# Seven moves in the schedule of an attention kernel: padding later, dividing sooner, one output product moved to the front of its place

## The chip, the cores and the metric

The program runs on one core of one Trainium2 chip. The metric is device time in microseconds (us), the median of three runs. Five engines work side by side, each in the order of its own instruction list: TensorE (PE; its weight loads are shown as PEld), VectorE (DVE), ScalarE (ACT), GpSimd (POOL), and SyncE (SP), which issues most transfers. [...] The order in which the program emits instructions is therefore the order in which each engine must do them, and a wait at the head of one list holds up everything behind it. Lines are cited as L and a number, which is the line of the kernel before.

## What is computed

The input is x of shape (4, 256, 48, 48) in 32-bit floats: four images of 256 channels and 2304 positions. Four layers follow, each added to its input; the first three read a group normalisation of it.

```python
x = x + L0(gn(x))   # 8-head attention over 2304 positions, q and k normalised; w_out, bias
x = x + L1(gn(x))   # gate: 3x3 max pool, blur with stride 3 to 16x16, depthwise taps, sigmoid, upsampled
x = x + L2(gn(x))   # one-head non-local attention, then a batch norm over all images
x = x + L3(x)       # channel gate, depthwise 3x3 convolution, instance norm, leaky relu

# the core of L0, for each image and head
sim  = einsum('bhdi,bhdj->bhij', q, k) * 10.0
out  = einsum('bhij,bhdj->bhid', softmax(sim), v)
y    = einsum('oc,bchw->bohw', w_out, out) + b_out

# the core of L1
t    = blur_pool(max_pool_3x3(gn(x)), stride=3)          # 16x16
gate = sigmoid(bn(dw(t, w_h1) + dw(t, w_v1) + diagonal taps of t))
y    = gn(x) * upsample(gate)
```

Layer 1 becomes 81 taps of a 16x16 tile that has a border of zeros (the padded tile).

## The kernel before, the parts concerned

Layer 0 is 16 phases, one for each image b and pair of heads p. A phase is six units of 384 query positions each, and a unit is nine groups of two blocks of 128 keys: 54 groups to a phase. Layer 2 follows with four phases of 27 groups. All other work (projections of the next pair, layer 1 of the image before, statistics) is given out to the groups. Within a group the emission order is this:

```python
for t, (u, g, st) in enumerate(groups):
    for j in range(g * G, (g + 1) * G):
        scores(u, j)                  # PE: scores (L238) into one of 2 "sc" tiles; ACT: exp (L244) -> pt
    if prev is not None:
        add_up(*prev)                 # DVE and POOL: row sums of exp (L284, L269)
    do(due, t)                        # small steps that are due, e.g. invert, divide
    do(fills, t)                      # PE work at fixed groups, sorted by the number it comes with
    ...
    for lane in st["others"]:         # generators: layer 1, group norms, follow
        gen, n, a, z, done, ready = lane
        until = -(-n * (st["at"] + 1 - a) // (z - a))
        clock["final"] = final = st["at"] == z - 1
        while final or (done < until and t >= ready and not ends):
            wait = next(gen, None)    # a yielded number: groups to wait
            if wait is None:
                break
            done, ready = done + 1, t + wait
    if prev is not None:
        ... weigh(pu, j)              # PE: exp times values (L258), of the group before
        if pg == NG - 1:
            last(pu, t)               # ends a unit
    prev = (u, g)
```

The end of a unit, counted in groups after its last weighing:

```python
AT_TOTAL, AT_FOLD, AT_INVERT, AT_DIVIDE, AT_AFTER = 3, 2, 6, 10, 11

def last(u, t):
    take(u)                                                      # ACT: copy out of PSUM
    ...
    todo = [
        (fills, AT_TOTAL, lambda: total(u)),                     # PE, ACT, SP: sums to a small tile l6
        (due, AT_FOLD, lambda: fold(u, nc.gpsimd)),              # POOL (L335)
        (due, AT_INVERT, lambda: invert(u)),                     # DVE (L311, L312), SP: rinv to 128 rows
        (due, AT_DIVIDE, lambda: divide(u, nc.gpsimd)),          # POOL: o = o * rinv (L339)
    ]
    after = AT_AFTER
    todo += [(fills, after, fn) for fn in u["after"]]            # the two output products
```

The group with number 2 in each unit (11 after the end of the last one) is the place of the 128-row products. The projection of the next pair stands there with the numbers 1, 2 and 3, and the output products beside it:

```python
def out_proj(b, p, c, pair, o):
    def part(k):
        ps = pj_tile()                                           # one of 2 "pj" banks
        nc.tensor.matmul(ps[:, :SL], lhsT=wo[...], rhs=o["o"], start=True, stop=True)        # L568
        xs = X[b][:, k, cols]
        nc.vector.scalar_tensor_tensor(xs, ps[:, :SL], pair["bo"][...], xs, ALU.add, ALU.add)  # L573
    return [((2.5, 4)[k], lambda k=k: part(k)) for k in range(NK)]

def chunk(s):              # qk: PE L502, evicted by ACT; values: PE L518, evicted by ACT
    def end():
        qk(s, 1)
        if s + 2 < NCH:
            fetch(s + 2)
    return [(1, lambda: qk(s, 0)), (2, lambda: values(s)), (3, end)]
```

Every `pj_tile()` takes the next of two banks in turn and has to wait until the reader of the one before last is done with it.

Layer 1 of image b runs beside the attention of image b + 1 and a little beyond it:

```python
TURNS, ROUND, HASTE = (2, 2, 3, 5, 6, 8), -1, -2      # groups of a unit in which a step may be taken
ROUND_TURNS = {ROUND: (2, 5, 8), HASTE: (2, 4, 6, 8)}

def padded(k, norm, res):
    pd = lp.tile([P, AS + 2 * PAD, AS + 2 * PAD], F32, tag="pd", name="pd")
    nc.gpsimd.memset(pd, 0.0)                                                    # POOL L724
    rs64 = lp.tile([P, 1], F32, tag="rs64", name="rs64")
    nc.vector.tensor_scalar(rs64, norm["rs"][:, k : k + 1], 1.0 / 64.0, ...)     # DVE L726
    nc.scalar.activation(pd[inner], res["blur"], AF.Identity, bias=..., scale=rs64)  # ACT L727
    return pd

def strips(b, k, norm, res):
    haste = HASTE if (b, k) == (NX - 1, NK - 1) else ROUND
    pd = padded(k, norm, res)
    ...
    products(0)            # ACT: 5 taps (L747)
    yield haste
    products(1)            # ACT: 4 taps
    yield haste
    for n, taps in enumerate(ROUNDS):      # 20 rounds
        ...                # ACT: products(n + 2); DVE: tensor_reduce (L765)
        yield haste

def l1_all(b):
    ...                    # statistics of the group norm, first half of the maxima
    for k in range(NK):
        if k:
            res = {}
            yield from maxima(b, k, res)       # DVE: 12 steps of max and blur, the last L708 to L715
        yield from strips(b, k, norm, res)
        yield from gated(b, k, norm, res)
        ...
    yield from gn(b, norm2, [1])               # statistics for layer 2

def follow(start, slices, norm):               # projection of the last image of layer 2
    while "nb" not in norm:
        yield 1
    start()                                    # PE L889, L895 on norm["nb"]
    yield 1
    for c in range(L2C):
        ...
```

And where the phases are set up:

```python
if (b, p) == (2, 0):
    for s in range(NSL):
        work.setdefault(s + 2 * NG, []).append(lambda s=s: send(s))      # X[0] to DRAM
        work.setdefault(s + 3 * NG, []).append(lambda s=s: receive(s))   # image 3 into its place
if b > 1 and p == 0:
    others.append((l1[b - 2], 10**6, 0, 2 * NG))     # rest of layer 1 of the image before last
```

Of the kernel before, what the change touches and what calls it, by code (L numbers as in the profile page):

```python
# [17 lines left out]
NK = 2  # L18
# [46 lines left out]
NG = JB // G  # L65
# [9 lines left out]
def usual_path(  # L75
# [15 lines left out]
    def pj_tile():  # L91
        return ps_pj.tile([P, 512], F32, tag="pj", name="pj")
# [5 lines left out]
    NX = B - 1  # L98
# [259 lines left out]
        nc.vector.tensor_tensor(lmin[:, 0:1], lmin[:, 0:1], two[:, 1:2], ALU.min)  # L358

    due, fills, clock = {}, {}, {}  # L360
    AT_TOTAL, AT_FOLD, AT_INVERT, AT_DIVIDE, AT_AFTER = 3, 2, 6, 10, 11

    def last(u, t):

# [197 lines left out]
    def out_proj(b, p, c, pair, o):  # L562

        cols = slice(c * SL, (c + 1) * SL)

        def part(k):
            ps = pj_tile()
            nc.tensor.matmul(  # L568
                ps[:, :SL], lhsT=wo[:, p, k * P : (k + 1) * P], rhs=o["o"], start=True,
                stop=True,  # L570
            )
            xs = X[b][:, k, cols]
            nc.vector.scalar_tensor_tensor(  # L573
                xs, ps[:, :SL], pair["bo"][:, k : k + 1], xs, ALU.add, ALU.add
            )

        return [((2.5, 4)[k], lambda k=k: part(k)) for k in range(NK)]

    def l0_unit(b, p, c, pair):
        hold = {}  # L580

        def o_tile():
            hold["o"] = op.tile([P, SL], F32, tag="o", name="o")
            return hold["o"]

        return {
            "pt": {}, "qc": slice(c * SL, (c + 1) * SL), "paired": PAIRED,
            "soon": b == B - 1 and p == NPAIR - 1 and c == NCH - 1,
            "scale": 1.0, "of": pair, "o": o_tile,
            "after": out_proj(b, p, c, pair, hold),  # L590
        }
# [60 lines left out]
    TURNS, ROUND, HASTE = (2, 2, 3, 5, 6, 8), -1, -2  # L652
    ROUND_TURNS = {ROUND: (2, 5, 8), HASTE: (2, 4, 6, 8)}

    def paced(gen):

        at, count, wait, turns = -9, 0, 0, TURNS
        while True:
            t, slot = clock["t"], clock["slot"]
            count = count if t == at else 0  # L660
            if not clock["final"] and (t < at + wait or count >= turns.count(slot)):
                yield 1
                continue
            wait = next(gen, None)
            if wait is None:
                return
            at, count = t, count + 1
            turns = ROUND_TURNS.get(wait, TURNS)
            yield 0
# [51 lines left out]
    def padded(k, norm, res):  # L721

        pd = lp.tile([P, AS + 2 * PAD, AS + 2 * PAD], F32, tag="pd", name="pd")
        nc.gpsimd.memset(pd, 0.0)  # L724
        rs64 = lp.tile([P, 1], F32, tag="rs64", name="rs64")
        nc.vector.tensor_scalar(rs64, norm["rs"][:, k : k + 1], 1.0 / 64.0, None, ALU.mult)  # L726
        nc.scalar.activation(  # L727
            pd[:, PAD : PAD + AS, PAD : PAD + AS], res["blur"], AF.Identity,
            bias=norm["nb"][:, k : k + 1], scale=rs64,
        )  # L730
        return pd

    def strips(b, k, norm, res):


        haste = HASTE if (b, k) == (NX - 1, NK - 1) else ROUND
        pd = padded(k, norm, res)

        bufs = [
            lp.tile([P, L1_BUF], F32, tag=tag, name="prod").rearrange("p (n s) -> p n s", s=NT + 1)  # L740
            for tag in ("t1", "t2", "t3")
        ]

        def products(n):
            for i, t in enumerate(ROUNDS[n]):
                dr, dc = TAPS[t]
                nc.scalar.activation(  # L747
                    bufs[n % 3][:, :, min(n, 1) + i].rearrange("p (r c) -> p r c", c=AS),
                    pd[:, PAD + dr : PAD + dr + AS, PAD + dc : PAD + dc + AS],
                    AF.Identity, scale=wt[:, k, t : t + 1],  # L750
                )

        products(0)
        yield haste
        products(1)
        yield haste
        for n, taps in enumerate(ROUNDS):
            last = n == len(ROUNDS) - 1
            if n + 2 < len(ROUNDS):
                products(n + 2)  # L760
            to = bufs[(n + 1) % 3][:, :, 0]
            if last:
                res["acc"] = lp.tile([P, AS, AS], F32, tag="l1acc", name="l1acc")
                to = res["acc"].rearrange("p r c -> p (r c)")
            nc.vector.tensor_reduce(  # L765
                to, bufs[n % 3][:, :, : min(n, 1) + len(taps)], AX.X, ALU.add
            )
            yield haste
# [246 lines left out]
    def l1_all(b):  # L1015

        norm, norm2 = norms1[b], norms2[b]
        norm2["st"] = small.tile([P, NK, NSL, 6], F32, tag="gn_st2", name="gn_st2")
        start = clock["t"]
        ahead = gn(b, norm)  # L1020
        for _ in range(NSL - 1):
            yield next(ahead)
        res = {}
        tops = maxima(b, 0, res)
        for _ in range(6):
            yield next(tops)

        while clock["t"] < start + NG + 2:
            yield 1
        yield from ahead  # L1030
        yield from tops
        for k in range(NK):
            if k:
                res = {}
                yield from maxima(b, k, res)
            yield from strips(b, k, norm, res)
            yield from gated(b, k, norm, res)
            if k == 0:
                for s in range(NSL):
                    nc.vector.bn_stats(norm2["st"][:, k, s, :], X[b][:, k, s * SL : (s + 1) * SL])  # L1040
                    if s % 2:
                        yield 0
        yield from gn(b, norm2, [1])
# [42 lines left out]
    l1 = [paced(l1_all(b)) for b in range(NX)]  # L1086
# [3 lines left out]
    def part(gen, n, last):  # L1090
        while n > 0 or last:
            wait = next(gen, None)
            if wait is None:
                return
            n -= 1
            yield wait
# [6 lines left out]
    def follow(start, slices, norm):  # L1103

        while "nb" not in norm:
            yield 1
        start()
        yield 1
        for c in range(L2C):
            while clock["t"] in taken:  # L1110
                yield 1
            for _, fn in slices[c] + slices[c + L2C]:
                fn()
            yield 1
# [6 lines left out]
    def send(s):  # L1121
        cols = slice(s * SL, (s + 1) * SL)
        nc.sync.dma_start(x_out[:, :, cols], X[0][:, :, cols])

    def receive(s):
        cols = slice(s * SL, (s + 1) * SL)
        nc.sync.dma_start(X[NX][:, :, cols], xv[:, :, NX, cols])
# [10 lines left out]
    for i, (b, p) in enumerate(order):  # L1138
        work, others = {}, []
        if i + 1 < len(order):  # L1140
            new = projs[i + 1]
            work[0] = [new["start"]]
            for s in range(NCH):
                work[NG * s + AT_CHUNK] = new["chunk"](s)
            work[NG + AT_CHUNK].append(new["out_bias"])
            for slot, fn in zip((n - 5, n - 3, n - 2, n - 1), new["scale"]):
                work[slot] = [fn]
            if i + 2 < len(order):
                work[n // 2] = [projs[i + 2]["prefetch"]]
                work[NG * (NCH - 1) + AT_CHUNK].append(projs[i + 2]["norms"])  # L1150
        else:
            start, slices = project2(0, norms2[0], twos[0])
            work[1] = [start]
            for s in range(NSL):
                work[NG * s + AT_CHUNK] = slices[s]
        if (b, p) == (2, 0):
            for s in range(NSL):
                work.setdefault(s + 2 * NG, []).append(lambda s=s: send(s))
                work.setdefault(s + 3 * NG, []).append(lambda s=s: receive(s))
        if (b, p) == (0, 0):  # L1160
            others.append((tap_weights(), WEIGHT_TICKS, 2, n - 2))
        if b > 0:
            end = n - 2 if (b, p) == (B - 1, NPAIR - 1) else n + 1
            others.append((l1[b - 1], 10**6, 2 if p == 0 else 0, end))
        if b > 1 and p == 0:
            others.append((l1[b - 2], 10**6, 0, 2 * NG))
        if (b, p) == (B - 1, NPAIR - 1):
            others.append((part(ahead, L1_AHEAD, False), L1_AHEAD, n - L1_AHEAD - 3, n))
        if p == 1 and b + 1 < B:
            others.append((gn(b + 1, norms0[b + 1]), GN_TICKS, 0, n - 2))  # L1170
        phases.append(([l0_unit(b, p, c, pairs[b][p]) for c in range(NCH)], work, others))

    n = L2C * NG
    for b in range(B):
        work, others = {}, []
# [1257 lines left out]
```

## Time and profile before

| quantity | before |
|---|---|
| median of 3 runs | 3723.43 us |
| lowest and highest | 3720.27 and 3728.46 us |
| span of the profiled run | 3718.2 us |
| PE busy | 3525.9 us, 95% |
| DVE busy | 2513.3 us, 68% |
| ACT busy | 2358.7 us, 63% |
| POOL busy | 1417.3 us, 38% |
| mean granted TensorE clock | 0.978 |

Busy time is how long an engine had an instruction of the program in it. The granted clock is the share of its full speed that TensorE was given. In lists of groups the columns are line, engine, operation, written and read tiles, shape and count, then busy time, mean nanoseconds of one, and the idle time of that engine just before them with what ended it. In a timeline each row is one instruction or a merged run of equal ones: start, duration, engine, line, operation, tiles, count, and in brackets the idle time before it and what ended it. A list of waits has the waiting engine, tile and line, an arrow to what it waited for, and then the total in us, how often, and the longest.

### The profile page before, as it was taken

To read this page: it belongs to the slowest core of one execution; us is meant where nothing else is said; L and a number is where in the kernel's file an instruction comes from. 1 tells how busy PE (TensorE), PEld (TensorE's weight loads), DVE (VectorE), ACT (ScalarE), POOL (GpSimd) and SP (SyncE) were. 2 spreads that over 40 slices of the span, in tenths; PEclk is the share of its full clock that TensorE was granted. 3 is DMA by queue.
4 is the path that set the end of the run, shared out by engine and by line. 5 is a ranking of instruction groups with operands and counts; after the bars stand their busy time and mean duration, and the time that the engine had idled before them with its cause. 6 is when DMAs were issued, how large, how long until landed. Compare 5 with 4: busy or idle time off the path is not lost.

```text
span 3718.2 us, 86544 instructions
## 1 busy us (share of the span) xinstructions
PE 3525.9 (95%) x36330; PEld 1770.1 (48%) x36330; DVE 2513.3 (68%) x3203; ACT 2358.7 (63%) x3819; POOL 1417.3 (38%) x900
## 2 busy tenths in 40 slices
PE   7999999999999999999999999999999999989685
PEld 4444545544445444444454444444444445655343
DVE  2455555476768666866686668666877886575687
ACT  5665666656776677567766775677678655545353
POOL 2333333333334333333343334333433456664242
PEclk9999999999999999999999999999999999999797
DMA  4111111111111111121111111111111100000001
GB/s 140 21 25 21 26 21 25 21 25 21 25 21 26 20 25 21 33 64 25 21 25 21 25 21 24 22 25 21 25 16 24 18 4 8 6 7 5 26 29 74
DMA packets 114591, 97.89 MB, mean 26 GB/s; under 512 B 56224, under 2 KB 111632, under 8 KB 112400
## 3 DMA queue, kind: packets, MB, share of 16 engines
q1 hardware_dynamic: 111728, 91.27, 12.9%
q8 instruction: 286, 4.69, 0.5%
q10 hardware_dynamic: 2464, 1.00, 0.1%
q14 instruction: 113, 0.93, 0.1%
HBM read 59.33 MB, written 11.80 MB: 19 GB/s over the span
## 4 chain that ended last, share of the span: by engine, by line
PE 76%; DVE 13%; issue 4%; ACT 2%; DMA 2%; POOL 2%; SPq 0%; DVEq 0%; POOLq 0%; ACTq 0%
PE sc L238 29%; PE av L258 29%; PE pj L502 7%; DVE acc L284 4%; PE pj L568 3%; PE pj L518 3%; DVE sc L1423 2%; DMA rinv<-rinv 1%; PE pj L291 1%; DVE av L1423 1%; PE pj L809 1%; POOL half L269 1%; DVE z L1472 1%; PE pj L925 1%; DVE gn_st L174 1%
## 5 line engine op out<-in xcount | busy, mean ns | idle before, releaser
L244 ACT ACTIVATE pt<-sc 128x768 f32<-128x768 f32 x1944 | 1477.3, 812 | 843.0 <-PE sc L238 833.8
L269 POOL TENSOR_TENSOR half<-pt 128x768 f32<-128x768 f32 x477 | 950.9, 1994 | 1619.4 <-ACT pt L244 1567.9
L238 PE MATMUL sc<-q,k 64*64 64x384 f32 x13824 | 1286.9, 488 | 31.9 <-ACT pt L244 29.4
L258 PE MATMUL av<-pt,v 64*64 64x384 f32 x13824 | 1285.1, 487 | 0.0
L284 DVE TENSOR_TENSOR acc<-acc,pt 128x768 f32<-128x768 f32 x792 | 876.1, 1106 | 103.2 <-ACT pt L244 20.6
L238 PEld LDWEIGHTS sc<-q,k 64*64 64x64 f32 x13824 | 516.2, 134 | 657.1 <-issue 515.9
L258 PEld LDWEIGHTS av<-pt,v 64*64 64x64 f32 x13824 | 517.5, 134 | 595.1 <-issue 558.8
L284 DVE TENSOR_TENSOR acc<-acc,half 128x768 f32<-128x768 f32 x459 | 476.9, 1039 | 296.7 <-POOL half L269 295.3
L573 DVE SCALAR_TENSOR_TENSOR x<-pj,bo,x 128x384 f32<-128x384 f32 x192 | 118.5, 618 | 566.1 <-PE pj L568 565.9
L502 PE MATMUL pj<-xs,w 128*128 128x384 f32 (+1 forms) x768 | 298.2, 512 | 1.7 <-issue 1.7
L747 ACT ACTIVATE prod<-pd,wt 128x256 f32<-128x256 f32 x486 | 280.4, 742 | 0.2
L339 POOL TENSOR_TENSOR o<-o,rinv 128x384 f32<-128x384 f32 x95 | 120.6, 1270 | 370.4 <-DMA rinv<-rinv 341.6
L502 PEld LDWEIGHTS pj<-xs,w 128*128 128x128 f32 x768 | 131.8, 190 | 153.9 <-issue 53.5
L258 PE MATMUL av<-pt,qv 64*64 64x384 f32 x1728 | 176.5, 500 | 0.0
L238 PE MATMUL sc<-qv,kd 64*64 64x384 f32 x1728 | 172.0, 490 | 3.9 <-ACT pt L244 3.9
L568 PE MATMUL pj<-o,wo 128*128 128x384 f32 x384 | 156.4, 492 | 16.4 <-POOL o L339 12.1
L765 DVE TENSOR_REDUCE prod<-prod 128x256 f32<-128x1280 f32 x114 | 168.7, 1480 | 0.0
L518 PEld LDWEIGHTS pj<-w,xs 128*128 128x128 f32 x1152 | 143.9, 192 | 25.9 <-issue 0.6
L278 DVE TENSOR_TENSOR acc<-pt 128x768 f32<-128x768 f32 x99 | 123.6, 1248 | 30.6 <-ACT pt L244 30.5
L518 PE MATMUL pj<-w,xs 128*128 128x128 f32 x1152 | 144.1, 275 | 0.0
L508 ACT ACTIVATE k<-pj,bias 128x384 f32<-128x384 f32 x96 | 55.7, 580 | 137.8 <-PE pj L502 137.3
L238 PEld LDWEIGHTS sc<-qv,kd 64*64 64x64 f32 x1728 | 80.2, 136 | 69.0 <-issue 53.0
(226 smaller groups left out, 2688.3 us busy)
## 6 DMA issues: line engine op xcount, KB each, us to landing
xs<-in_x_dram SPq DMA_DIRECT2D x96, 384.0 KB
rinv<-rinv SPq DMA_DIRECT2D x208, 94.5 KB
x<-in_x_dram SPq DMA_DIRECT2D x6, 1152.0 KB
out_dram<-x SPq DMA_DIRECT2D x6, 1152.0 KB
l<-row SPq DMA_DIRECT2D x416, 1.5 KB
w<-in_wqkv_dram SPq DMA_DIRECT2D x32, 192.0 KB
rinv<-ls SPq DMA_DIRECT2D x208, 1.5 KB
x_out<-x SPq DMA_DIRECT2D x6, 384.0 KB
```

Source lines behind the costliest of these rows:

```text
L238: nc.tensor.matmul(ps[c * D : (c + 1) * D, h, :SL], lhsT=u["of"]["k"][r, j0 : j0 + D], rhs=u["of"]["q"][r, u["qc"]], start=True, stop=True,)
L244: nc.scalar.activation(pt, ps[:, :, :SL], AF.Exp, scale=u["scale"])
L258: nc.tensor.matmul(u["av"][h * D : (h + 1) * D, half, :SL], lhsT=value(u, j, h)[r], rhs=pt[r, h, :], start=j == 0, stop=j == JB - 1,)
L269: nc.gpsimd.tensor_add(half, pts[0], pts[1])
L278: nc.vector.tensor_add(u["acc"], ready[0], ready[1])
L284: nc.vector.tensor_add(u["acc"], u["acc"], term)
L339: eng.tensor_mul(o, o, u["rinv"])
L502: nc.tensor.matmul(ps[:, :n], lhsT=at["w"][:, k, t, :], rhs=xs[s][:, k, :n], start=k == 0, stop=k == NK - 1,)
L518: nc.tensor.matmul(ps[:, i * P : (i + 1) * P], lhsT=xs[s][:, k, i * P : (i + 1) * P], rhs=at["w"][:, k, 2, :], start=k == 0, stop=k == NK - 1,
L568: nc.tensor.matmul(ps[:, :SL], lhsT=wo[:, p, k * P : (k + 1) * P], rhs=o["o"], start=True, stop=True,)
L747: nc.scalar.activation(bufs[n % 3][:, :, min(n, 1) + i].rearrange("p (r c) -> p r c", c=AS), pd[:, PAD + dr : PAD + dr + AS, PAD + dc : PA ...
L765: nc.vector.tensor_reduce(to, bufs[n % 3][:, :, : min(n, 1) + len(taps)], AX.X, ALU.add)
```

## The change

It moves seven things and computes the same. The sums of a unit are inverted, and its output divided, one group sooner. The first of the two output products goes to the front of the 128-row place. Layer 1 waits three groups between the last step of a blur and the padded tile made from it, so that ACT does not meet a tile that is not there yet. Because this makes layer 1 longer, the last layer-1 image goes at the quicker pace for both channel halves, and the rest of an earlier image may reach nine groups further into the next image; the reload of X[0] moves along by nine groups. Last, the projection for the last image of layer 2 starts two groups after its norm is there.

```diff
-    AT_TOTAL, AT_FOLD, AT_INVERT, AT_DIVIDE, AT_AFTER = 3, 2, 6, 10, 11
+    AT_TOTAL, AT_FOLD, AT_INVERT, AT_DIVIDE, AT_AFTER = 3, 2, 5, 9, 11
@@ out_proj
-        return [((2.5, 4)[k], lambda k=k: part(k)) for k in range(NK)]
+        return [(4 * k, lambda k=k: part(k)) for k in range(NK)]
@@ strips
-        haste = HASTE if (b, k) == (NX - 1, NK - 1) else ROUND
+        haste = HASTE if b == NX - 1 else ROUND
@@ l1_all
                 yield from maxima(b, k, res)
+
+            yield 3
             yield from strips(b, k, norm, res)
@@ follow
         while "nb" not in norm:
             yield 1
+        yield 2
         start()
@@ phases
-                work.setdefault(s + 3 * NG, []).append(lambda s=s: receive(s))
+                work.setdefault(s + 4 * NG, []).append(lambda s=s: receive(s))
@@
-            others.append((l1[b - 2], 10**6, 0, 2 * NG))
+            others.append((l1[b - 2], 10**6, 0, 3 * NG))
```

## The prediction

> **What bounds the kernel now.** I read the engines' busy shares first, then the list of TensorE's waits, then timelines around the longest. TensorE is busy for 3525.9 of 3718.2 us, and in an ordinary group it does scores and weighing back to back in 2.6 us. So only TensorE's idle stretches, and the slow clock after them, can be won.
>
> TensorE's own waits:
>
> ```profile
> engine line waited for: us in total, times, longest us
> PE sc L238 <- ACT pt L244: 33.3, 9, 4.8
> PE pj L568 <- POOL o L339: 12.1, 7, 2.9
> PE pj L889 <- DVE gn_nb L201: 7.2, 1, 7.2
> PE pj L192 <- DVE gn_sq L189: 5.3, 4, 2.0
> ```
>
> Six of the nine waits for exp lie in layer 0 and are 28.9 us of the 33.3, each 4.8 us. TensorE around one of them:
>
> ```profile
> 1648.15 1.47 PE L238 MATMUL sc<-q,k 64*64 64x384 f32 x16
> 1649.44 1.47 PE L258 MATMUL av<-pt,v 64*64 64x384 f32 x16
> 1655.72 2.84 PE L238 MATMUL sc<-q,k 64*64 64x384 f32 x16 [4.81 <-ACT pt L244]
> 1658.34 2.79 PE L258 MATMUL av<-pt,v 64*64 64x384 f32 x16
> ```
>
> The reader is to see the wait and that the next two runs take 2.8 us instead of 1.47: the granted clock is 0.75 over the 13.8 us from the wait's start, which is 6.9 us at half speed. ACT at the same time:
>
> ```profile
> 1647.22 0.87 ACT L300 COPY row<-pj 128x384 f32<-128x384 f32 x2
> 1651.63 0.60 ACT L727 ACTIVATE pd<-blur,gn_nb,rs 128x256 f32<-128x256 f32 x1 [3.54 <-DVE rs L726]
> 1652.27 2.76 ACT L747 ACTIVATE prod<-pd,wt 128x256 f32<-128x256 f32 x5
> 1654.84 1.53 ACT L244 ACTIVATE pt<-sc 128x768 f32<-128x768 f32 x2
> ```
>
> ACT stands 3.54 us before the padded tile, because VectorE reaches the tiny scale late, behind two steps of the blur and the row sums. Exp stands behind the tile and its five products.
>
> The second thing to read is the 128-row place while VectorE is behind. TensorE there, and VectorE there:
>
> ```profile
> 1200.32 1.47 PE L238 MATMUL sc<-q,k 64*64 64x384 f32 x16
> 1201.72 1.56 PE L502 MATMUL pj<-xs,w 128*128 128x384 f32 x4
> 1203.12 1.50 PE L518 MATMUL pj<-w,xs 128*128 128x128 f32 x12
> 1204.45 0.81 PE L568 MATMUL pj<-o,wo 128*128 128x384 f32 x2
> 1205.19 1.56 PE L502 MATMUL pj<-xs,w 128*128 128x384 f32 x4
> ```
>
> ```profile
> 1200.45 2.63 DVE L284 TENSOR_TENSOR acc<-acc,pt 128x768 f32<-128x768 f32 x2
> 1203.00 2.58 DVE L278 TENSOR_TENSOR acc<-pt 128x768 f32<-128x768 f32 x1
> 1205.50 0.60 DVE L573 SCALAR_TENSOR_TENSOR x<-pj,bo,x 128x384 f32<-128x384 f32 x1
> 1207.43 0.62 DVE L573 SCALAR_TENSOR_TENSOR x<-pj,bo,x 128x384 f32<-128x384 f32 x1 [1.32 <-PE pj L568]
> ```
>
> VectorE is free for the first output product only 5.2 us after the place begins. Today nothing waits for that: the product ends at about 4.9 us, and its bank is wanted again at 6.3 us.
>
> [...] half-speed stretches come as 3.4 us or twice that, after gaps of 4.8 us always, after one of two gaps of 2.0 us. [...] Here six gaps repeat; their cause is an order, not a buffer, but two banks for the small products are what I fear below. [...] acc<-acc,half takes 0.95 us alone and 2.58 us beside a GpSimd addition, so VectorE's lag has a cause that the change leaves.
>
> **Part by part.** The groups follow from the turns by counting, here from the start of the image's first phase. Half 0: the last step of the blur is in group 38; the pause is taken at the next turn, 39, and runs to 42, which is a turn. Half 1: 21 turns of one in three groups from 44 bring the gate to 107 instead of 104; its steps and the next maxima end in 141, the pause is taken at 143 and runs to 146, group 38 of the third phase.
>
> Padded tile. The wait costs 4.8 us, and the half-clock stretches behind the six are 3.4, 6.8, 6.8, 3.4, 6.8 and 6.8 us. Half of their 34 us is lost: 28.9 + 17 = 46; the lengths of the groups give 44, which I take. For half 0 the tile moves from group 39 to 42. VectorE has only row sums in between, so the 3.54 us go. What stays is ACT's own burst: 4.81 - 3.54 = 1.27 us, since 0.60 + 2.76 us beside 1.51 us of exp do not fit in 2.6 us. Three times 1.2 is 3.6. For half 1 of images 0 and 1 the tile moves from group 30 to 38, a 128-row place of 8.3 us; about 0.5 us remains each, 1 together. For image 2 at the quick pace it falls on group 23 and the next products on 24: about 4 us. Together 9 of 44 stay: **35 us saved**.
>
> Invert and divide. They start 2.6 us sooner, and where VectorE lags by more, because invert now stands ahead of a blur step (823.9 us in the trace would become 820.4). Seven waits of the output product, 12.1 us, should go: **12 us saved**.
>
> Output product at the front. It now wants the divided o 2.8 us sooner (4.13 us into the place becomes about 1.4), which about uses up the 2.6 us gained; in ordinary units the division ends 0.2 us before the place, so this is safe. But the banks are handed out in turn. Before: qk, values, output, qk, output. After: output, qk, values, qk, output. The values product now takes the bank of the output product, so it waits for VectorE's addition. It would start 3.6 us into the place; with VectorE free at 5.2 and 0.6 us for the addition, it waits 2.2 us. In the 22 units of image 0 VectorE is free in time. In images 1 to 3 the trace shows it free later than 2.9 us in 25 of 72 places, mostly 3.5 to 5.2. Counted with the new places of the blur and gate steps, I get 7 + 11 + 12 us for the three images: **30 us lost**. This is an estimate from the old lag.
>
> Longer reach of the earlier image. The tail of images 0 and 1 (statistics, then two small products) moves from groups 2 to 11 to groups 8 to 20, on top of the next image's first maxima. Its two waits (L192, 4.1 us and 1.7 us of slow clock) become perhaps 10: **4 us lost**.
>
> Projection of the last image. TensorE waits 7.2 us for its norm, and 10.2 us of half clock follow, 5 us lost. Two groups later is 6.4 us later, and GpSimd, which now stands 3.5 us for the reciprocal just there, is free sooner: **11 us saved**. The three groups that follow do not move, since the two groups skipped were closed to it anyway.
>
> Layer 2's padded tiles wait for GpSimd's memset behind a division (3.94 and 2.76 us); the earlier division brings some 1.5 us each and less slow clock: **4 us**. The quick pace and the later reload change the order only; small waits in the last phase give 1 us.
>
> Sum: 35 + 12 - 30 - 4 + 11 + 4 + 1 = 29 us. 3723 - 29 = **3694 us**.
>
> **Rivals.** One: the bank wait does not show, because VectorE has caught up by then. Then 30 us more are won: about 3665. For it speaks that some maxima steps move; against it, that the lag in group 38 of each image's first phase comes from steps which do not move. Two: VectorE or ACT becomes the bound in the crowded groups (layer-1 tail on new maxima, two padded bursts at the quick pace), [...]: 20 to 30 us more lost, about 3720. VectorE's share of 68% speaks against it as a whole; in those nine groups my count is over 30 us of work in 30 us. Three: the reciprocal's transfers, not the group in which they are asked for, set the division. From the inversion at 823.88 to the multiplication at 833.72 are 9.8 us, and GpSimd waits 10.2 us. Then dividing sooner only moves GpSimd's wait, and with the product at the front the seven waits stay or grow: about 3710.
>
> **Range and chances.** The gains of the padded tile and the late projection, 46 us, are read from gaps that are there; the losses are counted and may be off by half, 15 us either way, and rival two is open. So 3672 to 3716 at 8 in 10. Two per cent is 74 us: all gains without any loss are 63 us. Faster by over 2%: 0.03; within 2%: 0.95; slower by over 2%: 0.02.
>
> **What would show it.** Right: the six 4.8 us waits are gone, with 0.5 to 2.5 us left at most; L889 has no wait; a new wait of values (L518) for VectorE's x stands in the list with some 20 to 35 us. Wrong: no such wait (rival one), waits of L568 that are as long as before (rival three), or waits of L182 and L192 over 12 us and a lower granted clock around the start of images 2 and 3 (rival two).

## The result and the profile after

The changed kernel takes 3756.73 us (3754.57 to 3760.11), the kernel before, beside it on the same chip, 3723.39 us. The ratio is 1.0089 with a 95% interval of 1.0072 to 1.0107: 33 us slower, where 29 us faster was predicted.

The engines' busy shares after, the line that answers to the shares quoted in the prediction:

```profile
PE 3527.9 (94%) x36330; PEld 1780.1 (47%) x36330; DVE 2588.6 (69%) x3203; ACT 2360.3 (63%) x3819; POOL 1454.9 (39%) x900
```

TensorE's work is the same (3525.9 us before). VectorE does the same 3203 instructions in 75 us more (2513.3 us before). Keep that number in mind; its cause is the main finding.

TensorE's own waits after (us in total, times, longest):

```profile
PE pj L518 <- DVE x L573: 55.2, 27, 4.5
PE pj L182 <- DVE gn_mv L179: 19.7, 3, 17.2
...
PE sc L238 <- ACT pt L244: 11.8, 10, 2.4
PE pj L568 <- POOL o L339: 9.3, 10, 1.9
PE pj L973 <- DVE bst L981: 8.0, 5, 4.5
...
PE pj L925 <- DVE bst L981: 6.5, 3, 4.0
PE pj L192 <- DVE gn_sq L189: 6.0, 3, 2.6
...
PE pj L889 <- DVE bst L981: 3.2, 1, 3.2
```

The 33.3 us for exp fell to 11.8, as meant. At the top stands a wait that the kernel before did not have: the values product (L518) waits for VectorE's addition to x (L573), 55.2 us in 27 places. The output product's wait for o (L568) only fell from 12.1 to 9.3 us. L889 no longer waits for its norm but for VectorE's statistics (bst), which hold its bank.

One place with the new wait, TensorE first:

```profile
991.01 1.47 PE L238 MATMUL sc<-q,k 64*64 64x384 f32 x16
992.41 0.91 PE L568 MATMUL pj<-o,wo 128*128 128x384 f32 x2
993.16 1.45 PE L502 MATMUL pj<-xs,w 128*128 128x384 f32 x4
995.60 1.60 PE L518 MATMUL pj<-w,xs 128*128 128x128 f32 x12 [0.98 <-DVE x L573]
997.04 1.46 PE L502 MATMUL pj<-xs,w 128*128 128x384 f32 x4
998.33 0.81 PE L568 MATMUL pj<-o,wo 128*128 128x384 f32 x2
```

The new order is output, qk, values, qk, output. The output product is done at 993.3, but its bank is handed to the values product only when VectorE has added it to x. VectorE up to then, and below it GpSimd:

```profile
977.66 1.79 DVE L311 TENSOR_TENSOR ls<-l 128x6 f32<-128x6 f32 x1
...
988.97 2.63 DVE L284 TENSOR_TENSOR acc<-acc,pt 128x768 f32<-128x768 f32 x2
991.53 2.56 DVE L278 TENSOR_TENSOR acc<-pt 128x768 f32<-128x768 f32 x1
994.02 1.00 DVE L174 BATCH_NORM_STATS2 gn_st<-x 128x6 f32<-128x384 f32 x2
994.95 0.59 DVE L573 SCALAR_TENSOR_TENSOR x<-pj,bo,x 128x384 f32<-128x384 f32 x1
```

```profile
977.52 1.90 POOL L269 TENSOR_TENSOR half<-pt 128x768 f32<-128x768 f32 x1 [2.91 <-ACT pt L244]
...
989.10 1.69 POOL L339 TENSOR_TENSOR o<-o,rinv 128x384 f32<-128x384 f32 x1 [4.37 <-DMA rinv<-rinv]
991.11 2.17 POOL L269 TENSOR_TENSOR half<-pt 128x768 f32<-128x768 f32 x1 [0.32 <-ACT pt L244]
```

VectorE's first step of the inversion (L311, six numbers to a partition) takes 1.79 us here, from 977.66, while GpSimd adds exp tiles from 977.52. The steps behind it then slide into GpSimd's division and its next addition: the row sum at 991.53 takes 2.56 us. So VectorE reaches the addition to x 3.94 us into the place instead of well before it. In the kernel before, at the same unit, the same two lines read:

```profile
977.36 0.15 DVE L311 TENSOR_TENSOR ls<-l 128x6 f32<-128x6 f32 x1
986.37 0.96 DVE L278 TENSOR_TENSOR acc<-pt 128x768 f32<-128x768 f32 x1 [0.72 <-ACT pt L244]
```

The place began at 988.4 there, and VectorE was free 0.16 us before it. Nearly all of both steps ran clear of GpSimd.

This unit is no exception. Wherever L311 starts while a GpSimd operation runs, it ends with that operation, 0.02 to 0.03 us after it, though no semaphore ties the two: in all 31 such cases of the changed kernel, and in 36 of 39 in the kernel before (in the other three the operation was over within 0.04 us and L311 took 0.15 us). What the move changes is how much of the operation is left. Before, 30 of the 39 start more than 1.0 us after it, most of them behind VectorE's reduction L765, and take 0.15 to 0.83 us; in the changed kernel all 31 start within 0.9 us of it, each behind a row addition (L284), and take 1.55 to 1.80 us.

The padded tile, in its new place (ACT, then TensorE):

```profile
913.12 1.51 ACT L244 ACTIVATE pt<-sc 128x768 f32<-128x768 f32 x2 [1.01 <-PE sc L238]
915.59 0.61 ACT L727 ACTIVATE pd<-blur,gn_nb,rs 128x256 f32<-128x256 f32 x1 [0.95 <-DVE rs L726]
916.23 2.81 ACT L747 ACTIVATE prod<-pd,wt 128x256 f32<-128x256 f32 x5
918.84 1.52 ACT L244 ACTIVATE pt<-sc 128x768 f32<-128x768 f32 x2
```

```profile
919.73 1.56 PE L238 MATMUL sc<-q,k 64*64 64x384 f32 x16 [2.16 <-ACT pt L244]
```

A wait of 4.81 us has become 2.16 us: about 1.2 us is ACT's own burst, as predicted, and 0.95 us is ACT still waiting for the scale, because VectorE now does the inversion and 3.45 us of row sums just ahead of it. No slow clock follows here; behind one of the two waits like it (it ends at 1681.6 us) 3.4 us do.

### The profile page after: what moved, and what is told of

It reads as the page before. It is cut to its first block, busy times and chain, and to the rows that moved or that the text cites. A ratio compares the mean times of both kernels' runs of the same rounds, so it can differ in the third digit from the quotient of the medians.

```text
span 3756.4 us, 86478 instructions
## 1 busy us (share of the span) xinstructions
PE 3527.9 (94%) x36330; PEld 1780.1 (47%) x36330; DVE 2588.6 (69%) x3203; ACT 2360.3 (63%) x3819; POOL 1454.9 (39%) x900
## 4 chain that ended last, share of the span: by engine, by line
PE 63%; DVE 25%; issue 5%; ACT 4%; POOL 2%; DMA 1%; DVEq 0%; SPq 0%; ACTq 0%; POOLq 0%
PE sc L238 23%; PE av L258 23%; DVE acc L284 10%; PE pj L502 5%; PE pj L518 4%; PE pj L568 3%; DVE sc L1426 2%; DVE acc L278 2%; PE pj L291 1%; DVE av L1426 1%; ACT pt L244 1%; POOL half L269 1%; ACT prod L747 1%; DVE gn_st L174 1%; PE pj L809 1%
## 5 line engine op out<-in xcount | busy, mean ns | idle before, releaser
L269 POOL TENSOR_TENSOR half<-pt 128x768 f32<-128x768 f32 x477 | 963.7, 2022 | 1681.8 <-ACT pt L244 1620.6
L284 DVE TENSOR_TENSOR acc<-acc,pt 128x768 f32<-128x768 f32 x792 | 919.0, 1160 | 86.9 <-DVE acc L284 2.7
L284 DVE TENSOR_TENSOR acc<-acc,half 128x768 f32<-128x768 f32 x459 | 467.1, 1018 | 302.5 <-POOL half L269 300.7
L573 DVE SCALAR_TENSOR_TENSOR x<-pj,bo,x 128x384 f32<-128x384 f32 x192 | 118.1, 615 | 557.2 <-PE pj L568 557.2
L502 PE MATMUL pj<-xs,w 128*128 128x384 f32 (+1 forms) x768 | 286.5, 497 | 1.7 <-issue 1.7
L518 PE MATMUL pj<-w,xs 128*128 128x128 f32 x1152 | 155.3, 287 | 55.2 <-DVE x L573 55.2
L518 PEld LDWEIGHTS pj<-w,xs 128*128 128x128 f32 x1152 | 148.7, 200 | 91.5 <-DVE x L573 73.8
L502 PEld LDWEIGHTS pj<-xs,w 128*128 128x128 f32 x768 | 141.9, 196 | 80.9 <-issue 6.5
L568 PE MATMUL pj<-o,wo 128*128 128x384 f32 x384 | 166.3, 515 | 13.2 <-POOL o L339 9.3
L765 DVE TENSOR_REDUCE prod<-prod 128x256 f32<-128x1280 f32 x114 | 168.6, 1479 | 0.0
L278 DVE TENSOR_TENSOR acc<-pt 128x768 f32<-128x768 f32 x99 | 138.9, 1403 | 18.2 <-ACT pt L244 18.2
L508 ACT ACTIVATE q<-pj,bias 128x384 f32<-128x384 f32 x96 | 55.8, 581 | 98.5 <-PE pj L502 97.7
L335 POOL TENSOR_TENSOR o<-raw 128x384 f32<-128x384 f32 x95 | 115.9, 1220 | 0.0
```

Source lines behind the costliest of these rows:

```text
L269: nc.gpsimd.tensor_add(half, pts[0], pts[1])
L278: nc.vector.tensor_add(u["acc"], ready[0], ready[1])
L284: nc.vector.tensor_add(u["acc"], u["acc"], term)
L502: nc.tensor.matmul(ps[:, :n], lhsT=at["w"][:, k, t, :], rhs=xs[s][:, k, :n], start=k == 0, stop=k == NK - 1,)
L518: nc.tensor.matmul(ps[:, i * P : (i + 1) * P], lhsT=xs[s][:, k, i * P : (i + 1) * P], rhs=at["w"][:, k, 2, :], start=k == 0, stop=k == NK - 1,
L568: nc.tensor.matmul(ps[:, :SL], lhsT=wo[:, p, k * P : (k + 1) * P], rhs=o["o"], start=True, stop=True,)
```

## The experiments

Each time is the median of several executions, with the ratio to the kernel before on the same chip and its 95% interval. Cuts are marked @@; e7 and e8 are edits of e3, e12 one of e8.

**e1: the changed kernel with the old order of the place.**

```diff
-        return [(4 * k, lambda k=k: part(k)) for k in range(NK)]
+        return [((2.5, 4)[k], lambda k=k: part(k)) for k in range(NK)]
```

> The changed kernel with the first output product back at its old number, 2.5. Bank theory (the values product waits for VectorE to free the bank of the output product): the 55 us of L518 waits go and with them some 15 us of half clock; the second qk product waits again for ACT's copy of the values, 0.19 us in about 90 places, 17 us; so 3757 - 70 + 17 = about 3704, between 3690 and 3715. Crowding theory (the moved layer-1 work puts VectorE so far behind that TensorE waits for it wherever the product stands): 3735 or more, with the waits of L568 and L502 grown instead.

3699.75 us, ratio 0.9933 (0.9912 to 0.9954). The move to the front therefore costs 1.0089 - 0.9933 = 1.56% or 58 us in this kernel, and the other moves together win 25. The wait of L518 is gone. Two of its waits:

```profile
PE pj L568 <- DVE x L573: 10.4, 7, 2.1
PE pj L925 <- DVE bst L981: 6.6, 3, 4.0
```

Even in the old order VectorE's lateness shows a little: the second output product waits for the bank of the first.

**e2: the kernel before with only the new order of the place.**

```diff
-        return [((2.5, 4)[k], lambda k=k: part(k)) for k in range(NK)]
+        return [(4 * k, lambda k=k: part(k)) for k in range(NK)]
```

> The kernel before with only the output product moved to the front. Bank theory: VectorE's old lag gives L518 waits of 35 to 45 us, the undivided output adds to L568 since it is wanted 2.8 us sooner (12 becomes 25 to 35 us), 17 us are won at the second qk: together 20 to 45 us slower, 3743 to 3768. Crowding theory: without the moved layer-1 work the front place is harmless and wins its 17 us, about 3706.

3772.07 us, ratio 1.0120 (1.0100 to 1.0141), a little above the expectation. Two waits stand where one was expected to lead:

```profile
PE pj L568 <- POOL o L339: 37.7, 16, 6.1
...
PE pj L518 <- DVE x L573: 19.0, 14, 2.0
```

The front product comes before its o is divided, and while TensorE waits for o, VectorE catches up. So the 19.0 us are not yet a measure of VectorE's lag.

**e3: the changed kernel, but ACT frees the bank of the front product.** ACT copies it to SBUF and VectorE adds from there.

```diff
+            src = ps[:, :SL]
+            if k == 0:
+                src = rpool.tile([P, SL], F32, tag="first", name="first")
+                nc.scalar.copy(src, ps[:, :SL])
             nc.vector.scalar_tensor_tensor(
-                xs, ps[:, :SL], pair["bo"][:, k : k + 1], xs, ALU.add, ALU.add
+                xs, src, pair["bo"][:, k : k + 1], xs, ALU.add, ALU.add
```

> The changed kernel; ACT copies the first output product out of its bank and VectorE adds from that copy, so the bank no longer waits for VectorE. Bank theory: L518 waits for x vanish, the 17 us at the second qk stay won, ACT's extra 0.48 us per unit is hidden: about 3687, some 15 us under the run with the old place. Crowding theory: 3735 or more. If ACT is the tight one in these places, waits of L238 for exp grow from 12 us to over 30.

3679.93 us, ratio 0.9876 (0.9854 to 0.9898). No product waits for x in layer 0. All seven moves stay, the copies are added work, and the kernel is 2.1% faster than the changed one: the cost of the new order was the bank. From its list of waits:

```profile
PE pj L182 <- DVE gn_mv L179: 19.7, 3, 17.6
...
PE sc L238 <- ACT pt L244: 11.4, 9, 2.4
...
PE pj L568 <- POOL o L339: 7.8, 10, 1.7
```

It also beats e1, which has the old order, by 0.6%, so the front place itself is worth something once its bank comes free in time. What it is worth is seen in the waits of weight loads. In the kernel before:

```profile
PEld pj L502 <- ACT v L523: 43.9, 82, 0.5
```

There the second qk follows the output product and takes the bank of the values, so its weight load waits for ACT's copy of the values, up to 0.5 us. In the changed kernel this line is gone. An undisturbed unit of image 0 became 0.19 us shorter (29.62 to 29.43 us), a phase of six 1.13 us, and 15 phases make 17 us. That is what the move was for, and the prediction had not seen it.

**e4: the kernel before with the layer-1 moves alone** (pause, quicker pace, longer reach, later reload).

```diff
+            yield 3
             yield from strips(b, k, norm, res)
@@
-        haste = HASTE if (b, k) == (NX - 1, NK - 1) else ROUND
+        haste = HASTE if b == NX - 1 else ROUND
@@
-                work.setdefault(s + 3 * NG, []).append(lambda s=s: receive(s))
+                work.setdefault(s + 4 * NG, []).append(lambda s=s: receive(s))
@@
-            others.append((l1[b - 2], 10**6, 0, 2 * NG))
+            others.append((l1[b - 2], 10**6, 0, 3 * NG))
```

> The kernel before with the layer-1 part alone: the pause before the padded tile, the quick pace for image 2, the longer reach and the later reload. Padding theory: the six waits of 4.8 us and their half clock shrink from 44 to about 12 us, the tail on the next image's maxima costs some 8: about 3699. Crowding theory: the layer-1 part itself is the loss, 3723 or more.

3705.31 us, ratio 0.9944 (0.9924 to 0.9965): 21 us faster, 13 to 28 by the interval. The wait for exp fell from 33.3 to 13.3 us.

**e5: the kernel before with only the sooner inversion and division.**

```diff
-    AT_TOTAL, AT_FOLD, AT_INVERT, AT_DIVIDE, AT_AFTER = 3, 2, 6, 10, 11
+    AT_TOTAL, AT_FOLD, AT_INVERT, AT_DIVIDE, AT_AFTER = 3, 2, 5, 9, 11
```

> The kernel before with only the inversion and the division a group sooner. If the division theory holds, most of the 12 us of L568 waits go and in layer 2 the inversion, now ahead of the statistics on VectorE, costs 3 to 5 us at L925: net 4 to 9 us faster, 3714 to 3720. If the transfers set the division (rival three of the prediction), L568 keeps 9 us or more and the time does not fall.

3714.64 us, ratio 0.9966 (0.9951 to 0.9982): 13 us faster, 7 to 18 by the interval. The wait of L568 for o fell from 12.1 to 1.7 us, so the third rival (the transfers set the division) falls. But the page has a second line to read:

```profile
PE 3527.8 (95%) x36330; PEld 1764.1 (48%) x36330; DVE 2605.5 (70%) x3203; ACT 2359.8 (64%) x3819; POOL 1448.4 (39%) x900
```

VectorE is busy 92 us longer than before with the same instructions. L311 takes over 1 us in 31 of 104 cases (9 before), and L284 and L278 on single tiles take 931.8 and 145.9 us (876.1 and 123.6 before). VectorE was free for the first output product later than 2.9 us into the place in 25 of 72 places before; here it is 33. In the old order hardly anything waits for that: L568 waits 4.7 us for x.

**e6: the changed kernel with the first output product between qk and values.**

```diff
-        return [(4 * k, lambda k=k: part(k)) for k in range(NK)]
+        return [((1.5, 4)[k], lambda k=k: part(k)) for k in range(NK)]
```

> The changed kernel with the first output product between the first qk product and the values (number 1.5). Bank theory: its bank is now wanted by the second qk, 1.4 us later than the values want it at the front; the front's waits, each cut by 1.4 us, leave 15 to 22 us at L502 for x; the values wait 0.1 to 0.2 us each for ACT's eviction of qk. So about 3705, 3695 to 3715. If it is not the bank but the earlier need for the divided output that costs, the time stays near 3740.

3738.54 us, ratio 1.0037 (1.0023 to 1.0051), 33 us above the 3705 expected. Two lists, TensorE's waits and those of its weight loads:

```profile
PE pj L502 <- DVE x L573: 24.7, 16, 3.3
```

```profile
PEld pj L518 <- ACT q L508: 57.9, 86, 0.8
```

The bank theory got its part right: the wait moved to the second qk, which now takes the front product's bank and comes one product later, and it fell from 55.2 to 24.7 us. What was missed is the other bank: values now takes that of the first qk with only a short product between them, so it waits up to 0.8 us for ACT's copy in nearly every place. An undisturbed unit takes 0.3 us more than in the changed kernel, some 27 us over 90 units.

**e7: e3 with the old inversion and division.**

```diff
-    AT_TOTAL, AT_FOLD, AT_INVERT, AT_DIVIDE, AT_AFTER = 3, 2, 5, 9, 11
+    AT_TOTAL, AT_FOLD, AT_INVERT, AT_DIVIDE, AT_AFTER = 3, 2, 6, 10, 11
```

> The changed kernel with the bank freed by ACT, but inversion and division back at 6 and 10. The front place wants the divided output 2.7 us sooner; if the sooner division is what pays for that, L568 waits for GpSimd grow from 8 to some 30 us with half clock behind the long ones: about 3680 + 25 = 3705. If the division hardly matters, as its small effect with the old place suggests, 3685.

3727.32 us, ratio 1.0009 (0.9999 to 1.0018). The direction is right, the size larger than expected:

```profile
PE pj L568 <- POOL o L339: 45.3, 15, 5.3
```

Sooner inversion and division together are worth 13 us with the old order (e5), and 1.3% or 49 us with the front place. Their worth and that of the front place cannot be told apart.

**e8: e3 with layer 2's inversion back in group 6 and the padded tile's scale computed ahead of the pause.**

```diff
-                (due, AT_INVERT, lambda: invert(u)),
+                (due, AT_INVERT + ("shift" in u["of"]), lambda: invert(u)),
@@ l1_all
+            scale64(k, norm, res)       # the L726 step, moved here out of padded()
             yield 3
```

> The changed kernel with the bank freed by ACT; in layer 2 the inversion stays a group later, and the scale of the padded tile is computed before the pause, not after it. The three waits of 2.1 us shrink by the 0.95 us that ACT stood for the scale, and in layer 2 the waits for bst shrink by some 4 us with their half clock: about 3680 - 3 - 5 = 3672. If neither matters, 3680.

3666.66 us, ratio 0.9841 (0.9824 to 0.9857). This is the fastest version: 1.6% below the kernel before and 2.5% below the changed one. The output product hardly waits for o:

```profile
PE pj L568 <- POOL o L339: 6.7, 9, 1.7
```

**e9: the kernel before with the new order and the sooner division, layer 1 as it was.** It settles whose lag the 55.2 us are.

```diff
-    AT_TOTAL, AT_FOLD, AT_INVERT, AT_DIVIDE, AT_AFTER = 3, 2, 6, 10, 11
+    AT_TOTAL, AT_FOLD, AT_INVERT, AT_DIVIDE, AT_AFTER = 3, 2, 5, 9, 11
@@ out_proj
-        return [((2.5, 4)[k], lambda k=k: part(k)) for k in range(NK)]
+        return [(4 * k, lambda k=k: part(k)) for k in range(NK)]
```

> The kernel before with only two of the seven moves: invert and divide a group sooner, and the output product at the front of the place. Layer 1 stays where it was, so VectorE lags as it did before. The move to the front without the sooner division hid part of the wait for VectorE behind a wait for the divided o (37.7 us at L568), so it did not measure the old lag cleanly; this run does. Theory one: the wait of values for VectorE's x grew to 55 us in the changed kernel because the later padding and the longer tail put more layer-1 work in front of the places. Then L518 waits here about the 30 us counted from the old lag, some 8 us of slow clock follow, the second qk wins 17 us, and sooner division 10 us: 3725 + 30 + 8 - 17 - 10 = 3736. Theory two: the old lag itself was counted too small, and the other moves have little part in it. Then L518 waits 50 us or more and the time is 3715 + 57 = about 3770, the 57 us being what the move costs in the changed kernel.

3773.05 us, ratio 1.0138 (1.0121 to 1.0156). My theory that the moved layer-1 work had made VectorE late falls:

```profile
PE pj L518 <- DVE x L573: 46.9, 25, 3.5
...
PE pj L568 <- POOL o L339: 14.7, 10, 3.8
```

With layer 1 untouched the wait is 46.9 of 55.2 us. Only about 8 us belong to the layer-1 moves. Against e2 the sole difference is the sooner inversion and division; its gain at L568 (37.7 to 14.7 us) is eaten by L518 (19.0 to 46.9 us).

**e10: the kernel before with only the later projection.**

```diff
         while "nb" not in norm:
             yield 1
+        yield 2
         start()
```

> The kernel before with only the later start of the last image's projection in layer 2. If the 7.2 us wait for the norm and the slow clock behind it are all that this costs, as the prediction had it, the time falls by about 11 us, to 3714, and L889 does not wait. If the two groups only bring the projection to a bank that VectorE's statistics still hold (bst), as in the changed kernel, where L889 waited 3.2 us and the phase was only 4.6 us shorter, the fall is about 5 us, to 3720. In the kernel before the inversion stands behind the statistics, not in front of them, so the first is the likelier of the two if the order of inversion and statistics is what makes the wait for bst.

3720.24 us, ratio 0.9996 (0.9985 to 1.0006): nothing that can be told from zero. The wait of 7.2 us at L889 is gone, but at the same spot two others stand: L973 for bst, 3.05 us, and L889 for bst, 1.15 us, with 6.8 us of slow clock instead of 10.2. The group after is reached only 2.5 us sooner. The expectation's first reading, that the order of inversion and statistics makes the wait for bst, falls for this place, since that order is unchanged here.

**e11: the changed kernel, inversion back in group 6, division left in group 9.**

```diff
-    AT_TOTAL, AT_FOLD, AT_INVERT, AT_DIVIDE, AT_AFTER = 3, 2, 5, 9, 11
+    AT_TOTAL, AT_FOLD, AT_INVERT, AT_DIVIDE, AT_AFTER = 3, 2, 6, 9, 11
```

> The changed kernel with the inversion back in group 6 and the division left in group 9. It asks which half of the sooner division made VectorE late. With only the sooner inversion and division, and the old order of the place, VectorE was free for the first output product later than 2.9 us in 33 of 72 places, before in 25, and the first tiny step of the inversion took over 1 us in 31 of 104 cases, before in 9: a group sooner it falls beside GpSimd's addition of exp tiles, and what follows is pushed into GpSimd's division. Theory one, the inversion's place on VectorE: here the long cases fall back to about 9, the waits of L518 for x from 55 us to about 35, with some 5 us less slow clock, while L568 waits perhaps 5 to 10 us more for o, since the transfers start up to a group later: about 3735 to 3745. Theory two, the division's place on GpSimd beside VectorE's row sums: that has not moved, so L518 still waits 50 us or more, and the time is 3757 or above it by what L568 waits more.

3759.00 us, ratio 1.0077 (1.0056 to 1.0098). Its busy line and its waits:

```profile
PE 3540.8 (94%) x36330; PEld 1786.1 (47%) x36330; DVE 2490.9 (66%) x3203; ACT 2360.4 (63%) x3819; POOL 1423.4 (38%) x900
```

```profile
PE pj L568 <- POOL o L339: 45.6, 13, 6.4
...
PE pj L518 <- DVE x L573: 17.9, 11, 3.5
```

The first theory holds for VectorE: the inversion's place alone takes 98 us off its busy time (2588.6 to 2490.9), L311 is long in 14 cases instead of 31, and VectorE is late in 22 of 72 places instead of some 32. The wait of L518 falls by 37 us, more than expected; a part of that is hidden behind L568, as in e2. But L568 then waits 45.6 us for o, not some 15 to 20, and the time is where it was. When the division is asked for, in group 9 or 10, hardly matters (45.6 here, 45.3 in e7); the inversion sets it.

**e12: e8 with layer 0's inversion in group 6.**

```diff
-                (due, AT_INVERT + ("shift" in u["of"]), lambda: invert(u)),
+                (due, AT_INVERT, lambda: invert(u)),
```

together with the edit of e11.

> The best version so far (ACT frees the front product's bank, layer 2 inverts in group 6, the padded tile's scale ahead of the pause) with layer 0's inversion in group 6 too, the division still in group 9. Here no product waits for VectorE's addition to free a bank, so a less late VectorE is worth little: if theory one holds, L568 waits some 5 to 15 us more for o, for a gain of at most 5 us elsewhere: about 3667 to 3677, against 3667 of the version with the inversion in group 5.

3729.23 us, ratio 1.0003 (0.9994 to 1.0011), more than 50 us above the expectation, for the same reason:

```profile
PE pj L568 <- POOL o L339: 46.5, 16, 5.6
```

Against e8 the only difference is that layer 0's inversion stands one group later. It costs 1.6%, about 60 us. Against e7, which divides in group 10, the wait is nearly the same.

The runs that vary the order of the place, side by side:

| kernel | order of the place | invert, divide | ratio | L518 for x, us | L568 for o, us |
|---|---|---|---|---|---|
| before | old | 6, 10 | 1 | none | 12.1 |
| e5 | old | 5, 9 | 0.9966 | none | 1.7 |
| e2 | front | 6, 10 | 1.0120 | 19.0 | 37.7 |
| e9 | front | 5, 9 | 1.0138 | 46.9 | 14.7 |
| changed | front, layer 1 moved | 5, 9 | 1.0089 | 55.2 | 9.3 |
| e11 | front, layer 1 moved | 6, 9 | 1.0077 | 17.9 | 45.6 |
| e1 | old, layer 1 moved | 5, 9 | 0.9933 | none | none |
| e3 | front, ACT frees, layer 1 moved | 5, 9 | 0.9876 | none | 7.8 |
| e7 | front, ACT frees, layer 1 moved | 6, 10 | 1.0009 | none | 45.3 |
| e8 | as e3, with its two edits | 5, 9 | 0.9841 | none | 6.7 |
| e12 | as e8 | 6, 9 | 1.0003 | none | 46.5 |

In the front place without ACT the two waits make 57 to 65 us in every row: o in time means VectorE late, and VectorE in time means o late. Only a bank that does not need VectorE, together with the sooner inversion, escapes both.

## Why the prediction was wrong, point by point

The sum was -59 us without the new order and +30 us for it. Measured: -25 us (e1) and +58 us. Of the 62 us between -29 and +33, the term of the front product accounts for 28, and the gains for 34: 11 at the padded tile, 3 at the division, about 10 at the late projection and about 10 that the parts win alone but not together.

- **Output product at the front: the step that failed.** Its mechanism was right, to the bank and the line: values waits for VectorE's addition, and the new wait stands first in the list. Its term was mis-sized: 30 us, "an estimate from the old lag". The waits are 55.2 us in 27 places. Behind seven of them lie 30.7 us of half clock, of which up to half is lost, 15 us, which the term did not have. L568 keeps 9.3 us of wait for o, and other waits for the same addition (L946) are 2.5 us. Off go the 17 us at the second qk, which I had overlooked, and the 10.4 us that e1 waits in the old order. That makes an estimate of 55.2 + 15 + 9.3 + 2.5 - 17 - 10.4 = 55 of the 58 us measured.
- **Why the old lag was the wrong one.** The lag that the term was read from did not stay. Of 72 places VectorE was late in 25 before and in 33 in e5, and above all it was later in them. For each of the 72 places I took how far VectorE's free moment plus 0.7 us lies beyond 3.6 us. The sum is about 36 us before, 64 in e5, 61 in e9, 71 in the changed kernel and 39 in e11 (a few us more or less, by the moment at which a place is taken to begin). The sooner inversion brings some 28 us of the rise, the moved layer 1 some 10. The prediction counted on the inversion coming "2.6 us sooner, and where VectorE lags by more", and asked only whether o would come in time. It had seen that VectorE's additions are slow beside GpSimd's (2.58 us instead of 0.95), but took this for "a cause that the change leaves"; the change moved a VectorE step into it. Two parts of the same change bore on each other, and I had costed them alone.
- **What lengthens VectorE's work.** That the inversion's place does it is shown by e5 (with the division) and by e11 and e12 (alone). That it is GpSimd's work beside it is read from the traces: every L311 of over 1 us ends with a GpSimd operation, 0.02 to 0.03 us after it. Not every step is stretched. In both kernels, beside a GpSimd operation or not, the reduction L765 takes 1.47 to 1.48 us, L573 0.59 to 0.62 us and the reciprocal L312 0.19 us; but the row sum L278 takes 0.93 to 2.59 us, and in the changed kernel the small copy L684 takes 0.18 to 0.19 us alone and 0.98 to 2.48 us beside GpSimd. What sets the stretched steps apart is not shown. No run took GpSimd's additions away, so this link rests on the traces, not on an experiment.
- **Padded tile.** The six long waits became three of 2.15 to 2.16 us and small ones; about 12 of the 44 us of group length are left, where 9 were predicted: about right. With the longer tail (4 us lost, about as predicted: L192 has two waits of 2.6 us with 3.4 us of slow clock each) 32 us were predicted for these moves and e4 measured 21 (13 to 28). In e4 L568 waits 1.9 us more for o than before; the rest of the gap was not traced.
- **Invert and divide.** 12 us, and 4 in layer 2; e5 gave 13: right, but only in the old order. In the whole change 9.3 of the 12.1 us of wait stayed, since the front place needs o 2.7 us sooner. In layer 2 the two waits behind GpSimd's memset shrank as predicted, from 3.94 and 2.76 to 2.41 and 1.75 us. Against that, the inversion now stands ahead of the statistics on VectorE, and L925 waits 6.5 us for them instead of 1.9. What that costs in time is not shown: the second phase of layer 2 took 136.9 us instead of 133.0, but 133.6 in e5, which has the same inversion, and 136.8 in e8, which has the old one there. So e8's 13 us over e3 are not layer 2's inversion alone: in the profiled runs some 9 us of the gain lie in layer 0, where only the padded tile's scale was moved, and 4 in layer 2.
- **Projection of the last image: the second step that failed.** 11 us predicted, nothing measurable in e10. The prediction took the norm for the only thing that TensorE waited for there. The wait for the norm was hiding a wait for a bank that VectorE's statistics hold; two groups later that one comes last (3.05 us at L973 and 1.15 us at L889 in e10).
- **The gains may not add.** The three groups of moves alone win 21, 13 and 1.5 us, together 25 and not 35. The intervals (13 to 28, 7 to 18, -2 to 6, and 17 to 33 for e1) leave room for no gap at all. The 10.4 us of L568 for x in e1, where e5 had 4.7 and the kernel before none, speak for one.
- **Rivals.** The first (no bank wait) falls by e1 and e3. The third (transfers set the division) falls for the old order by e5. It comes back in a changed form in the front place, where the inversion, and so the start of the transfers, sets the division. The second had the right engine, but its place was wrong: not the nine crowded groups of layer 1, whose waits are about as small as predicted (L192 6.0 us, and L182 2.5 us beside the one of 17 us that the kernel before has too), but the stretch from the inversion to the place. TensorE's mean clock stayed at 0.977 (0.978 before).

## What to carry to other kernels

When a product moves to an earlier place in a rotation of few banks, write down for every product whose read frees the bank that it will take, and give that read to an engine that is on time there; one small copy on ACT in each unit turned 0.9% slower into 1.2% faster. A lag read from the old trace holds only as long as no other part of the change touches the list of the engine that lags: even a step of six numbers, moved one group, made it late. Two moves that feed the same place are to be measured alone and together.

## What the runs showed of the hardware

- A VectorE addition of six numbers to a partition (L311) took 0.10 to 0.17 us alone. Where it started while GpSimd was at work, it ended 0.02 to 0.03 us after GpSimd did in 67 of 70 cases of the two kernels, and took up to 1.80 us. The row sum L278 took 0.94 to 0.96 us alone and up to 2.59 us beside GpSimd, while L765 and L573 kept their 1.48 and 0.62 us. With the same 3203 instructions VectorE's busy time was 2490.9 us (e11) or 2588.6 us (changed), by the place of one step.
- In the kernel before, the weight loads of L502 wait for ACT's copy of the values (43.9 us in 82 cases, up to 0.5 us), and no wait for that copy stands among its matmuls. Yet the order with that wait took 0.19 us more in an undisturbed unit (29.62 us against 29.43); the one with waits of up to 0.8 us (e6) took 0.3 us more than the changed kernel.
- The half clock did not follow the length of the gap alone. In the changed kernel a gap of 2.32 us at 895.1 us was followed by 3.4 us of slow clock from 897.9, while one of 2.53 us at 2419.0 us was followed by none:

```profile
897.37 2.48 PE L518 MATMUL pj<-w,xs 128*128 128x128 f32 x12 [2.32 <-DVE x L573]
2421.57 1.60 PE L518 MATMUL pj<-w,xs 128*128 128x128 f32 x12 [2.53 <-DVE x L573]
```

What differs is where the gaps lie. In the traces of the kernel before and of the changed one the slow stretches, 23 and 28 of them, begin whole multiples of 3.4133 us apart. Marked off from there in equal pieces of that length, the first gap lies whole in the piece from 894.5 to 897.9 us; the second is cut at 2420.2 into 1.2 and 1.3 us. From 60 to 3060 us of these two traces TensorE was idle for at least 2.03 us in 16 of the 19 full-speed pieces ahead of a slow stretch, and for at most 1.85 us in each of the 1712 others. The remaining three (1.23, 1.73 and 1.98 us) are not explained. No run moved a gap and nothing else, so this too rests on the traces.

The prediction's "half-speed stretches come as 3.4 us or twice that" holds for 19 of the 23 in the kernel before; the other four, from 3323.5 us on, last 10.2 to 28.4 us.
